# An opening with blank products, spare buffers and loads by need; the third group's norm one group of turns later

## The chip, the cores and the metric

The kernel runs on one core of one Trainium2 chip. The metric is device time in microseconds (us) of one execution of the whole program. Engines are named as in the profile: PE (TensorE matmul) with PEld (its weight loads), DVE (VectorE), ACT (ScalarE), POOL (GpSimd) and SP (SyncE, which only issues DMAs here; SPq in the profile). Each engine runs its own instructions in order and waits on semaphores for the others.

## The reference

Two layers over x of 64 sequences x 32 rows x 256 features, with a context of 64 x 257 x 256. Each of six steps adds a function of the normed x to x:

```
x = x + L0_xattn(layernorm(x), ctx)      # 16 heads of 16, rotary positions, causal window
x = x + L0_attn(layernorm(x))            # causal self attention, rotary positions
x = x + L0_ffn(layernorm(x))             # one product, rows scaled and rounded to fp8
x = x + L1_xattn(layernorm(x), ctx)      # full attention over 257 context rows
x = x + L1_attn(layernorm(x))            # gated mixer with a running sum
x = x + L1_ffn(layernorm(x))             # shared expert and the best 2 of 8 experts
```

The change lies in the first step. With everything else cut away it is

```
m = mean(x); v = var(x); n = (x - m) / sqrt(v + 1e-5)
q = rope(split(n   @ q_w.T + q_b)) * 16 ** -0.5
k = rope(split(ctx @ k_w.T + k_b));  v = split(ctx @ v_w.T + v_b)
e = exp(scores - max(scores)),  scores = q . k  for keys at or before the query, among the first 32
x = x + merge((e / sum(e)) @ v) @ o_w.T + o_b
```

where rope turns each head's halves (a, b) into (a cos - b sin, a sin + b cos).

## The kernel before

**Groups and turns.** The 2048 rows of x form four groups (NG) of 512; a group is four tiles (NT) of 128 rows, that is of four sequences. The two attentions of layer 0 run in one pipeline over `order`, eight items n: four groups of the cross attention, then four of the self attention. Each n has four turns t, and a turn handles one tile. The list `line` carries tiles through five stages, one per turn: `scores`, `sums`, `turned` with `context`, `by_feature`, `project`. In the turns of n the kernel also makes ready the next item, `after` (n + 1): its keys, queries and values, one projection per turn (`rotated`) and two value products (`values`). In the same turns the rows of n + 2 are normed by the generator `side` (`norm_steps`), which is advanced by `prepare`, and are transposed by `opened` at t = 3. All instructions of this stage are kept in program order on every engine, so the Python order is the order of each queue.

**Norm.** `norm_steps` takes the statistics on DVE (four bn_stats, four aggregates), starts an inverse square root with three integer steps (ve, half, r0), refines it with three Newton rounds and writes y = (x - m) r, a pair of tiles at a time. With `eng` vector a Newton round is three small DVE operations; without it, four small POOL operations. Each `yield` is a place where the caller can put other work.

**Rotary exchange.** `rotated(it, i, c)` makes half c of the keys (i = 1) or queries (i = 0): PE fills `ps_qk`, DVE writes `part` (times sine), SP issues four DMAs that copy `part` into `far` with its halves of 32 partitions swapped, `near` (times cosine) comes from DVE for n = 0 and from ACT and POOL for later n, and the function returned adds near and far on POOL into `kT` or `qT`. There are two buffers each of near and part (rings n0, n1 and p0, p1), three of far. `spread_keys` then writes `kT` into the block form `kb`, three heads on ACT and one on POOL, for half a group at a time.

**Values.** `values` writes two tiles to `v`, SP stores them to `v_rows` in HBM, and `blocks` loads them back as `vb` in four DMAs per half group. The parts of `vb` off the blocks must be zero: four clears (`clear`) at the start, two on DVE and two on POOL.

**Opening.** Before the loop (L500 to L537) the kernel loads x and the weights (`first_loads`, a generator whose steps are taken by `next(loads)`: three before the loop, then one in most turns), norms group 0, makes its keys, queries and values, norms group 1 and loads group 0's `vb`. Group 1's transposes (`opened(after)`) come in the turn (0, 0), group 2's in (0, 3). For n = 0 group 2's Newton rounds are on DVE; in later n on POOL. SP issues all loads but two, in program order, so a transfer behind an issue that waits is issued late.

Of the kernel before, what the change touches and what calls it, by code (L numbers as in the profile page):

```python
# [7 lines left out]
F32 = mybir.dt.float32  # L8
# [8 lines left out]
P = 128  # L17
# [48 lines left out]
def perceiver_kernel(ctx: ExitStack, tc: tile.TileContext, a: dict, out: bass.AP):  # L66
# [57 lines left out]
    def norm_steps(g, eng=None, apart=False, ts=range(NT), by_act=False):  # L124
# [18 lines left out]
        r = r0.bitcast(F32)  # L143
        for _ in range(3):
# [102 lines left out]
    def small_attentions(layers, first_loads, decode, sides, load_layer1, layer1):  # L247
# [30 lines left out]
        def clear(vb, engine):  # L278
            engine.memset(vb.rearrange("p b h g e -> p (b h g e)"), 0.0)
# [25 lines left out]
        def rotated(it, i, c):  # L305
# [19 lines left out]
            part = part_([P, GT], "part")  # L325
# [8 lines left out]
            near = near_([P, GT], "near")  # L334
# [166 lines left out]
        eye = sb.tile([P, S], BF16, tag="eye", name="eye")  # L501
        loads = first_loads()
# [4 lines left out]
        next(loads)  # L507
        for half in range(2):
            clear(vbs[0][half], vector)
            clear(vbs[1][half], gpsimd)  # L510
# [4 lines left out]
        adds = [rotated(it, 1, 0)]  # L515
# [3 lines left out]
        steps = norm_steps(order[1][1], vector, apart=True)  # L519
        next(steps)  # L520
        adds.append(rotated(it, 1, 1))
# [4 lines left out]
        adds.append(rotated(it, 0, 1))  # L526
        adds[1]()
# [4 lines left out]
        for pair in range(2):  # L532
            values(it, pair)
        after["y"] = finish(steps)
        for half in range(2):
            blocks(it, half)
        now = it  # L537


        line = [None] * 5  # L540
        adds = []
        layer1_loads = load_layer1()
        for n in range(len(order) + 1):
# [4 lines left out]
            kvT = coming = None  # L548
            if n + 2 <= last:
                side = norm_steps(order[n + 2][1], None if n else vector, apart=True)  # L550
            else:
                side = sides

            def prepare(at):
                if n + 2 <= last and at:
                    try:
                        next(side)
                    except StopIteration as end:
                        return end.value

            for t in range(NT):
# [9 lines left out]
                if t == 0:  # L571
# [9 lines left out]
                else:  # L581
                    y = prepare(t % 2 == 1)
                    adds.append(rotated(after, *((1, 0), (1, 1), (0, 0), (0, 1))[t]))
                if line[3]:
                    by_feature(line[3])
                prepare(t % 2 == 0)
# [13 lines left out]
                elif t % 2 == 0:  # L600
                    values(after, t // 2)
                    if (n, t) == (0, 0):
                        opened(after)
                elif t == 3:
                    for half in range(2):
                        blocks(after, half)
                    if n + 2 <= last:
                        coming = group(n + 2, kvT)
                        coming["y"] = y
                        opened(coming)  # L610
# [10 lines left out]
                if t == 0 and n + 2 <= last:  # L621
                    kvT = fetch(n + 2)
                elif n < 3:
# [1444 lines left out]
```

## Time and profile before

| what | us |
|---|---|
| runs, median (lowest to highest of 3) | 906.89 (904.85 to 907.39) |
| the profiled execution, its own time | 907.43 |
| its span from first to last instruction | 905.7 |
| first PE product | 8.16 |
| score products of groups 0, 1, 2 begin (mask product of the turn t = 0) | 30.85, 51.62, 75.51 |
| PE busy in 0 to 20, 20 to 40 | 11.84, 16.78 |
| PE busy in 104 to 128 (24.0) | 23.61 |

A profile line of an instruction gives start, duration, engine, source line, operation, output<-inputs, shape and count, and in brackets the idle time of the engine before it and what ended that time. L107 and L119 are helpers through which all engines' operations and all matrix products pass, so groups are told apart by the names of the tiles. A chain line gives start, duration and the engine or transfer that the end was waiting for at that time. The time of a DMA is from its issue to its landing.

### The profile page before, as it was taken

To read this page: it belongs to the slowest core of one execution; us is meant where nothing else is said; L and a number is where in the kernel's file an instruction comes from. 1 tells how busy PE (TensorE), PEld (TensorE's weight loads), DVE (VectorE), ACT (ScalarE), POOL (GpSimd) and SP (SyncE) were. 2 spreads that over 40 slices of the span, in tenths; PEclk is the share of its full clock that TensorE was granted. 3 is DMA by queue.
4 is the path that set the end of the run, shared out by engine and by line. 5 is a ranking of instruction groups with operands and counts; after the bars stand their busy time and mean duration, and the time that the engine had idled before them with its cause. 6 is when DMAs were issued, how large, how long until landed. Compare 5 with 4: busy or idle time off the path is not lost.

```text
span 905.7 us, 22825 instructions
## 1 busy us (share of the span) xinstructions
PE 852.7 (94%) x8699; PEld 587.2 (65%) x8699; DVE 583.9 (64%) x1706; ACT 437.8 (48%) x1129; POOL 505.7 (56%) x992
## 2 busy tenths in 40 slices
PE   6899999979899999999999999999898889999997
PEld 3466666656456666666666666565566548888886
DVE  7887777897677677774785766778765861111116
ACT  2567666654555554554555546655544232222224
POOL 3477777864774757564664648555652353555430
PEclk9999999999999999999999999999899999999999
DMA  7455433543110111111011113000001056776668
GB/s 241 136 143 136 100 90 104 135 118 106 54 54 4 52 54 54 54 54 54 7 49 54 54 54 100 3 1 2 25 25 36 24 160 193 238 237 232 215 188 284
DMA packets 66926, 88.77 MB, mean 98 GB/s; under 512 B 32480, under 2 KB 50688, under 8 KB 64768
## 3 DMA queue, kind: packets, MB, share of 16 engines
q1 hardware_dynamic: 63264, 77.73, 28.6%
q0 software_dynamic: 3456, 9.44, 3.1%
q8 instruction: 69, 1.13, 0.5%
q14 instruction: 41, 0.34, 0.1%
q10 hardware_dynamic: 96, 0.13, 0.1%
HBM read 65.78 MB, written 13.11 MB: 87 GB/s over the span
## 4 chain that ended last, share of the span: by engine, by line
PE 71%; DVE 15%; POOL 4%; ACT 4%; issue 3%; DMA 2%; SPq 0%; DVEq 0%; POOLq 0%; ACTq 0%
PE ps_v L119 12%; PE ps_o L119 11%; PE ps_k L119 10%; PE ps_h L119 7%; PE ps_t L122 7%; PE ps_qk L119 4%; PE ps_s L119 4%; PE ps_p L119 3%; PE ps_so L119 2%; PE ps_q L119 2%; PE pair_bank L119 1%; DVE y L107 1%; POOL sq L107 1%; ACT e L107 1%; PE psT L122 1%
## 5 line engine op out<-in xcount | busy, mean ns | idle before, releaser
L107 ACT ACTIVATE e<-e,xnm 128x257 f32<-128x257 f32 x256 | 127.2, 499 | 50.9 <-DVE xnm L107 41.0
L107 DVE CUSTOM_DVE_ANT_0 e<-ps_s,mask 128x257 f32<-128x257 f32 x256 | 93.5, 421 | 49.8 <-PE ps_s L119 49.5
L119 PE MATMUL ps_k<-ct,w_w_l1x 128*128 128x512 f32 x256 | 122.3, 600 | 1.6 <-ACT yT L107 0.6
L119 PE MATMUL ps_v<-w_w_l1x,ct 128*128 128x256 f32 x512 | 122.3, 382 | 0.0
L107 POOL TENSOR_SCALAR e<-e,xsm 128x256 f32<-128x256 f32 x256 | 121.3, 492 | 0.0
L122 PE MATMUL ps_t<-cst,e 128*128 128x128 f32 x640 | 102.7, 284 | 7.7 <-DVE eT L107 6.8
L107 DVE COPY eT<-ps_t 128x512 f32<-128x512 f32 x124 | 85.2, 687 | 28.6 <-PE ps_t L122 28.4
L119 PEld LDWEIGHTS ps_v<-w_w_l1x,ct 128*128 128x128 f32 x512 | 94.5, 193 | 11.0 <-issue 0.2
L107 ACT ACTIVATE kT<-ps_k,vec 128x512 f32<-128x512 f32 x64 | 44.0, 688 | 101.0 <-PE ps_k L119 100.7
L107 POOL TENSOR_TENSOR x<-x,rows 128x256 f32<-128x256 f32 x96 | 71.0, 755 | 37.3 <-ACT y L107 18.0
L122 PEld LDWEIGHTS ps_t<-cst,e 128*128 128x128 f32 x640 | 71.9, 142 | 26.2 <-DVE eT L107 7.7
L107 ACT ACTIVATE hTr<-ps_h,w 128x256 f32<-128x256 f32 (+1 forms) x80 | 31.4, 449 | 106.0 <-issue 82.7
L107 DVE TENSOR_TENSOR og<-ps_o,b 128x512 f32<-128x512 f32 (+1 forms) x20 | 12.8, 639 | 105.6 <-PE ps_o L119 105.6
L119 PEld LDWEIGHTS ps_k<-ct,w_w_l1x 128*128 128x128 f32 x256 | 44.6, 190 | 41.3 <-issue 35.2
L1811 POOL DMA_INDIRECT r_rows<-og,lv x36 | 35.5, 986 | 61.0 <-DVE og L107 56.1
L119 PE MATMUL ps_h<-ygT,w 128*128 128x256 f32 (+1 forms) x320 | 67.5, 365 | 0.1
L107 ACT COPY v<-ps_v 128x512 f32<-128x512 f32 x80 | 46.4, 581 | 39.2 <-PE ps_v L119 39.1
L119 PE MATMUL ps_o<-w,hTr 128*128 128x256 f32 x288 | 65.3, 379 | 0.0
L107 POOL TENSOR_TENSOR last<-e,xsm 128x4 f32<-128x4 f32 x64 | 12.9, 202 | 88.6 <-DVE xsm L107 88.6
L119 PEld LDWEIGHTS ps_h<-ygT,w 128*128 128x128 f32 x320 | 56.2, 194 | 6.6 <-issue 0.3
L119 PEld LDWEIGHTS ps_o<-w,hTr 128*128 128x128 f32 x288 | 54.5, 190 | 7.2
L107 ACT ACTIVATE kb<-kT,cst 128x256 f32<-128x256 f32 x96 | 45.4, 512 | 25.7 <-POOL kT L107 24.0
(210 smaller groups left out, 1667.1 us busy)
## 6 DMA issues: line engine op xcount, KB each, us to landing
ct<-in_ctxT SPq DMA_DIRECT2D x16, 1024.0 KB, 5.6
w<-in_ew SPq DMA_DIRECT2D x20, 514.0 KB, 4.1
w<-in_ew SPq DMA_DIRECT2D x20, 512.0 KB, 3.8
far<-part SPq DMA_DIRECT2D x126, 64.0 KB, 2.5
v_rows<-v SPq DMA_DIRECT2D x16, 256.0 KB, 2.3
vb<-v_rows SPq DMA_DIRECT2D x64, 64.0 KB, 2.3
r<-r_rows SPq DMA_DIRECT2D x8, 512.0 KB, 7.2
b<-in_eb SPq DMA_DIRECT2D x20, 128.0 KB, 3.7
```

The costliest lines, as they stand in the source:

```text
L107: ins = getattr(self.engine, name)(*args, **kw)
L119: return kept(nc.tensor.matmul(ps, **args))
L122: return kept(nc.tensor.transpose(ps, src, eye))
L1811: wrote = nc.gpsimd.indirect_dma_start(out=r_rows, out_offset=bass.IndirectOffsetOnAxis(ap=write_i[:, at : at + 1], axis=0), in_=o[:, i, : ...
```

## The change

The opening starts with 14 products of a zeroed bf16 tile `blank` into the PSUM bank b5, which nothing reads. All four clears of `vb` are on POOL. Both halves of group 0's keys are projected before its transposes; the first two `part` and `near` tiles are in the tiles that scores and exponentials use later (sc0, sc1, e0, e1), not in their rings. Group 1's norm gets one more place to pause. The loads of x2, w3, one bias row and the fp8 weights come after group 0's values; x3 and the later rows and weights come in later turns, and group 2's context in the turn (0, 1). The second half of group 0's `vb` is loaded in (0, 1). In the turns of n = 0 the adds stand first in each turn; group 1 is transposed in (0, 1). Group 2's statistics are taken in (0, 2), its Newton rounds in (0, 3), now on POOL, its y in (1, 0) and (1, 1), and its transposes in (1, 1).

```diff
@@ -121,7 +121,7 @@
     def turn(ps, src, eye):
         return kept(nc.tensor.transpose(ps, src, eye))
 
-    def norm_steps(g, eng=None, apart=False, ts=range(NT), by_act=False):
+    def norm_steps(g, eng=None, apart=False, ts=range(NT), by_act=False, split=False):
 
         x = xs[g]
         n, t0 = len(ts), ts[0]
@@ -141,6 +141,8 @@
         r0 = small.tile([P, n], I32, tag="r0", name="r0")
         vector.tensor_scalar(r0, half, -1.0, float(0x5F3759DF), ALU.mult, ALU.add)
         r = r0.bitcast(F32)
+        if split:
+            yield
         for _ in range(3):
             sq = small.tile([P, n], F32, tag="sq", name="sq", bufs=6)
             rn = small.tile([P, n], F32, tag="rn", name="rn", bufs=6)
@@ -275,8 +277,8 @@
             scalar.copy(mk, cst[:, at : at + S][:, None, :].to_broadcast([P, 8, S]))
             masks.append(mk)
 
-        def clear(vb, engine):
-            engine.memset(vb.rearrange("p b h g e -> p (b h g e)"), 0.0)
+        def clear(vb):
+            gpsimd.memset(vb.rearrange("p b h g e -> p (b h g e)"), 0.0)
 
         def fetch(n):
             layer, g = order[n]
@@ -322,7 +324,8 @@
                 return tile_.rearrange("p (b q) -> p b q", q=S)
 
             bias = vec[:, v0 + 2 * i + c : v0 + 2 * i + c + 1]
-            part = part_([P, GT], "part")
+            spare = (it["n"], i) == (0, 1)
+            part = sb.tile([P, GT], F32, tag=f"sc{c}", name="part") if spare else part_([P, GT], "part")
             vector.scalar_tensor_tensor(
                 by_seq(part), by_seq(ps), bias, by_place(sn), ALU.add, ALU.mult
             )
@@ -331,7 +334,7 @@
             for at in range(0, P, S):
                 queue = scalar if (it["n"], i, c) == (0, 0, 1) and at >= 2 * S else sync
                 queue.dma_start(out=far[at : at + S, :], in_=part[at ^ S : (at ^ S) + S, :])
-            near = near_([P, GT], "near")
+            near = sb.tile([P, GT], F32, tag=f"e{c}", name="near") if spare else near_([P, GT], "near")
             if it["n"] > 0:
                 scalar.activation(near, ps, AF.Identity, bias=bias)
                 gpsimd.tensor_tensor(by_seq(near), by_seq(near), by_place(cs), ALU.mult)
@@ -499,31 +502,35 @@
 
         kT_all = sb.tile([P, 2, GT], F32, tag=wide[4], name="kT")
         eye = sb.tile([P, S], BF16, tag="eye", name="eye")
+        blank = sb.tile([P, GT], BF16, tag="e2", name="blank")
+        vector.memset(blank, 0.0)
+        idle = psum.tile([P, GT], F32, tag="b5", name="idle")
+        for _ in range(14):
+            mm(idle, lhsT=blank[:, 0:P], rhs=blank, start=True, stop=True)
         loads = first_loads()
         next(loads)
         it = group(0, fetch(0))
         next(loads)
         after = group(1, fetch(1))
-        next(loads)
-        for half in range(2):
-            clear(vbs[0][half], vector)
-            clear(vbs[1][half], gpsimd)
+        for vb in vbs[0] + vbs[1]:
+            clear(vb)
         scalar.copy(ident_bf, ident)
         mask(0)
         it["y"] = finish(norm_steps(order[0][1], vector))
         it["kb"] = [None, None]
-        adds = [rotated(it, 1, 0)]
+        adds = [rotated(it, 1, c) for c in range(2)]
         opened(it)
         mask(1)
         vector.tensor_tensor(eye, ident[:, 0:S], ident[:, 64 : 64 + S], ALU.add)
-        steps = norm_steps(order[1][1], vector, apart=True)
+        steps = norm_steps(order[1][1], vector, apart=True, split=True)
         next(steps)
-        adds.append(rotated(it, 1, 1))
+        next(steps)
         adds[0]()
         for part in range(2):
             spread_keys(it, 0, 0, part)
         adds.append(rotated(it, 0, 0))
         adds.append(rotated(it, 0, 1))
+        next(steps)
         adds[1]()
         for part in range(2):
             spread_keys(it, 0, 1, part)
@@ -531,14 +538,14 @@
             add()
         for pair in range(2):
             values(it, pair)
+        next(loads)
+        next(loads)
+        blocks(it, 0)
         after["y"] = finish(steps)
-        for half in range(2):
-            blocks(it, half)
         now = it
 
-
         line = [None] * 5
-        adds = []
+        adds, side = [], None
         layer1_loads = load_layer1()
         for n in range(len(order) + 1):
             if n > 0:
@@ -546,17 +553,22 @@
             if after is not None:
                 after["kb"] = [None, None]
             kvT = coming = None
+            earlier = side
             if n + 2 <= last:
-                side = norm_steps(order[n + 2][1], None if n else vector, apart=True)
+                side = norm_steps(order[n + 2][1], apart=True)
             else:
                 side = sides
 
-            def prepare(at):
-                if n + 2 <= last and at:
+            def prepare(count):
+                y = None
+                for _ in range(count if n + 2 <= last else 0):
                     try:
                         next(side)
                     except StopIteration as end:
-                        return end.value
+                        y = end.value
+                return y
+
+            ahead, behind = ((0, 1, 0, 1), (1, 0, 1, 0)) if n else ((0, 0, 0, 1), (0, 0, 1, 0))
 
             for t in range(NT):
                 if line[2]:
@@ -568,7 +580,7 @@
                     elif after is not None:
                         kb_now = (after, 0, t - 2)
                 due, adds = adds, []
-                if t == 0:
+                if t == 0 or n == 0:
                     for add in due:
                         add()
                     due = []
@@ -579,11 +591,17 @@
                 if after is None:
                     next(layer1, None)
                 else:
-                    y = prepare(t % 2 == 1)
+                    if n == 1 and t == 0:
+                        next(earlier)
+                    elif n == 1 and t == 1:
+                        after["y"] = finish(earlier)
+                    y = prepare(ahead[t])
                     adds.append(rotated(after, *((1, 0), (1, 1), (0, 0), (0, 1))[t]))
+                    if n < 2 and t == 1:
+                        opened(after)
                 if line[3]:
                     by_feature(line[3])
-                prepare(t % 2 == 0)
+                prepare(behind[t])
                 if n + 2 > last:
                     next(side, None)
                     next(side, None)
@@ -599,15 +617,16 @@
                     next(layer1, None)
                 elif t % 2 == 0:
                     values(after, t // 2)
-                    if (n, t) == (0, 0):
-                        opened(after)
                 elif t == 3:
                     for half in range(2):
                         blocks(after, half)
                     if n + 2 <= last:
                         coming = group(n + 2, kvT)
-                        coming["y"] = y
-                        opened(coming)
+                        if n > 0:
+                            coming["y"] = y
+                            opened(coming)
+                if (n, t) == (0, 1):
+                    blocks(now, 1)
                 line[0] = scores(now, t) if n <= last else None
                 if (n, t) == (last, NT - 1):
                     pair_pool.close()
@@ -618,9 +637,9 @@
                     context(line[2])
                 if line[1]:
                     sums(line[1])
-                if t == 0 and n + 2 <= last:
+                if t == (0 if n else 1) and n + 2 <= last:
                     kvT = fetch(n + 2)
-                elif n < 3:
+                elif n < 3 and (n, t) != (0, 0):
                     next(loads, None)
                 elif n >= last - 2:
                     next(layer1_loads, None)
@@ -646,12 +665,15 @@
         sync.dma_start(out=xs[1], in_=x_view[1])
         yield
         sync.dma_start(out=xs[2], in_=x_view[2])
+        yield
         sync.dma_start(out=w_cur[:, 3], in_=a["w_l0x"][:, 3])
         row_load(R_XO0)
+        sync.dma_start(out=raw, in_=a["w_fp8"])
+        yield
         sync.dma_start(out=xs[3], in_=x_view[3])
         yield
-        sync.dma_start(out=raw, in_=a["w_fp8"])
-        for at in (R_AO0, R_FF, R_XO1, R_GO):
+        row_load(R_AO0)
+        for at in (R_FF, R_XO1, R_GO):
             yield
             row_load(at)
         for i in range(0, 4, 2):
```

## The prediction

> **What bounds the kernel now.** I read the page first, then busy time by stretches, then the opening in order of time, then the chain of waits up to 60 us.
>
> ```profile
> span 905.7 us, 22825 instructions
> ...
> PE 852.7 (94%) x8699; PEld 587.2 (65%) x8699; DVE 583.9 (64%) x1706; ACT 437.8 (48%) x1129; POOL 505.7 (56%) x992
> ...
> PE 71%; DVE 15%; POOL 4%; ACT 4%; issue 3%; DMA 2%; SPq 0%; DVEq 0%; POOLq 0%; ACTq 0%
> ```
>
> ```profile
> 20.00:30.80 10.80, 7.58 (x32) 4.71 (x30) 9.68 (x28) 4.85 (x12) 5.40 (x7) 1.00 0.53 139
> 30.80:51.60 20.80, 20.29 (x285) 12.74 (x284) 17.13 (x45) 14.32 (x32) 11.96 (x13) 0.92 0.46 126
> 51.60:75.20 23.60, 22.95 (x369) 16.11 (x368) 19.69 (x45) 15.44 (x36) 17.32 (x28) 1.00 0.51 134
> ...
> 80.00:104.00 24.00, 23.67 (x375) 16.03 (x372) 18.52 (x44) 15.72 (x36) 17.34 (x28) 1.00 0.54 134
> ```
>
> The columns are stretch, length, then busy time of PE, its weight loads, DVE, ACT, POOL, then granted clock. From 51.6 us on PE works 97 to 99% of each group's 23.6 to 24 us, so whatever PE starts earlier there is kept to the end. Spare time exists only before: 8.16 us until the first product, 3.2 us of the stretch 20 to 30.8, and a clock of 0.92.
>
> ```profile
> 8.16 3.75 PE L119 MATMUL ps_qk<-kvT,w_w_l0x 128*128 128x512 f32 x4 [8.16 <-DMA kvT<-in_ctx32T]
> ...
> 22.53 1.96 PE L119 MATMUL ps_qk<-kvT,w_w_l0x 128*128 128x512 f32 x4
> 24.33 1.99 PE L119 MATMUL ps_v<-w_w_l0x,kvT 128*128 128x256 f32 x8
> 27.93 0.78 PE L122 MATMUL psT<-cst,y 128*128 128x128 f32 x4 [1.61 <-DVE y L107]
> 30.24 0.68 PE L122 MATMUL psT<-cst,y 128*128 128x128 f32 x4 [1.53 <-ACT near L107]
> 30.85 0.41 PE L119 MATMUL pair_bank<-mk,eye 64*32 64x256 bf16 x8
> ```
>
> ```profile
> 14.64 3.52 DMA far<-part
> ...
> 18.29 1.28 POOL kT L107
> ...
> 26.95 2.55 issue
> 29.50 0.69 ACT near L107
> ```
>
> The same projection (four records) takes 3.75 us at the start and 1.96 later: PE starts at half speed, though the granted clock reads 1.00 there; durations decide. It is slow again after the idle time of 26.3 to 30.2: the clock row of 31 to 34 us is 0.50. The first score product of group 0 stands at 30.85; it waits for the exchange far (3.52 us instead of the median 2.3, behind 369 GB/s of loads), for the rotations one after another, and for PE's transposes of group 1, held by DVE.
>
> **Part 1, blank products.** PE's first instruction now needs only a DVE clear of 128x256 words; 2048 took 1.76 us, so under 0.3: start about 1.6 us. No row shows a 128x512 bf16 product. A 128x256 one is 0.13 (ps_ff, eight in 1.04 from 206.55), and bounds it below; four times that, twice the columns at half clock, is 0.52 above. So 14 take 1.8 to 7.3 us and end at 3.4 to 8.9. I take eight slow and six fast (8x0.52 + 6x0.26 = 5.7), end 7.3, before kvT lands at 8.03; the upper end costs 0.9 us of start. In this trace PE needed about 4.2 us of work to leave half speed (8.16 to 12.4, where the transposes quicken) and fell back after some 4.4 us with 0.8 us of work in them. The hole 7.3 to 8.16 is shorter. The Trainium skill, "TensorE: Matmul & The Clock Gate", What's actually happening, says the watching window is 3.4 us and free-running; by its 0.427 us a slow product all 14 would end at 7.6, and an unlucky window only shifts how many are slow.
>
> **Part 2, order up to the first score product.** PE: both key projections 2x1.8 from 8.16 to 11.8, transposes 1.3 to 13.1, ACT's second copy 0.58 to 13.7, queries 3.60 to 17.3, values 3.63 to 20.9, group 1's key and value projections 1.73 each to 24.4. The DVE clears (2x1.76) leave before the norm; four POOL clears (4x1.81 from 0.74) end at 8.0, and POOL was idle until 18.29. The spare part/near buffers remove two waits of queries on keys (1.34 <- DMA far, 0.50 and 0.60 <- POOL kT). Exchange side: part of the first keys at 10.3, its four issues (0.6 each) 11.1 to 13.5 with x2, w3, row and x3 no longer in front, landing 15.4; keys' adds 16.8 and 19.1; the queries' issues end 20.3 (two on ACT), landing 22.3, adds 22.4 and 23.7. So the first score product comes at 24.4, PE's own time, against 30.85: **-6.4**. Group 1's transposes (1.3) move behind it, and group 2's move out of group 0's turns, so PE's work in those turns stays equal.
>
> **Part 3, group 0's turns.** What is late next is SP's queue, which is full. ACT copies the values at 21.9; then SP issues v_rows (2), x2, w3, row, raw to 24.2, four vb 1.9, far of group 1's first keys 2.4 (to 28.6), v_rows 0.5, far 2.4, the other four vb 1.9, kvT 0.4, far of the first queries 2.4: to 36.2, landing about 38.2. On POOL behind it: query add 1.28 (39.5), key spread 0.5, and now group 2's Newton steps, twelve of 0.285 in pitch as the steps at 56.78 to 60.06 (43.4). They were DVE's before (nine at 0.2). Behind them wait the near product 1.28 (44.7) and the second query add (46.0), which group 1's first scores need. These stood at 51.62, so 5.6 of the 6.4 are left: **+0.8**. PE alone would be ready at 44.1.
>
> **Part 4, group 1's first turns.** In the chain before, DVE runs without a break from 49.78 (part) to 56.70, then near and cT on ACT, then ps_p at 58.85: 9.07 us. Added to it: the second pair of y, 2x0.39 = 0.79, and two yT copies (1.07) between near and cT: 10.9. It starts when the first pair of y is done, and that needs the Newton steps of 43.4. Rows bound it: free, y takes 0.8 (part at 44.2, ps_p at 55.1); blocked by POOL it does not.
>
> ```profile
> 43.44 1.26 DVE L107 TENSOR_SCALAR y<-x,mv,rn 128x256 f32<-128x256 f32 x2
> ...
> 62.41 1.25 DVE L107 TENSOR_SCALAR y<-x,mv,rn 128x256 f32<-128x256 f32 x2
> ```
>
> Both pairs began while a POOL add ran (42.95, 61.92) and waited for its end; here near and add follow at once, so y could end at 46.4 and ps_p come at 57.3. That is 3.7 or 1.5 before 58.85; I take the middle, 2.6: **+3.0**. The skill's "SBUF — State Buffer", Who interferes with whom, speaks against moving work to GpSimd here: whoever starts first holds the shared port for the whole instruction. By that rule alone POOL, in order on its own engine, wins, and the sum would be -1.5. PE's 1.3 us of transposes lies inside this wait.
>
> Loads that are put later: x3 is issued about 36.7 and must be there for group 3's statistics at about 45; w_l0a comes one or two slots later, three turns ahead of use. Both free; uncovered, x3 costs what it is late beyond 8 us (median landing 7.9 in the crowded opening).
>
> **Sum** -6.4 + 0.8 + 3.0 = -2.6 on the profiled execution's 907.43 (span 905.7 plus 1.7 around it) is 904.8. The median of the runs, 906.89, lies 0.54 below that execution, so I forecast 904.3 for the median.
>
> **Rivals.** A: everything is carried. POOL gets to near and the add before the Newton steps bind, or far lands earlier; then the half-clock stretch (3.02 against 1.88, 1.08 against 0.64, small ones: 1.7) is saved too, against 1.3 for transposes in a full group: -6.8, 900.1. For it: PE is the bound in 71% of the chain; against: SP's and POOL's queues above. B: the products don't warm PE (idle before kvT, or the wrong window). The first key pair and transposes run slow: 1.9 + 0.7, the whole chain of v_rows and SP starts 2.6 later, net 0: 906.9. Against it: the 4.2 us seen. C, slower: the exchange of the first queries lands as slowly as loads do, because kvT (512 KB) now stands right before it on SP; before it stood 3.3 us ahead. Price: x's median landing 7.9 less 2.3 = 5.6, straight down POOL to part 4, and PE idles 44 to 50, long enough to halve its clock again as at 30.7, 2.1 more: -2.6 + 7.7 = +5.1, 912.0. It eats the gain from 2.6 us of lateness and is measurably slower from 5.3. Against it: only one load of 512 KB is in flight there, and far at 37.20, 3.3 us behind the same load, showed no delay.
>
> **How the numbers follow.** Forecast (-1 to -5) 0.50, A 0.20, B 0.12, C 0.18. A change of 0.3% (2.7 us) is about what can be told from none: three fifths of the forecast's share and A are beyond it, 0.50; the rest of the forecast and B within, 0.32; C slower, 0.18. The likeliest case alone spans 901.9 to 905.9. The range reaches into A and past B: 900.3 to 908.0.
>
> **What would show it.** First projection in about 1.9 us at 8.2; first score product at 24 to 25; no clock row under 1.0 before 60; PE idle 1 to 2 us before group 1's first scores with POOL's add as releaser; y of group 2 with a mean over 0.6 us; ps_p near 56. Wrong if PE runs half clock at 8 to 12, if far after kvT lands later than 4 us, or if group 1's first turns take no longer than before.

## The result and the profile after

| | before | after |
|---|---|---|
| median of 22 runs each (lowest to highest), us | 906.29 (903.96 to 908.89) | 908.59 (906.03 to 913.52) |
| ratio, 95% interval | | 1.0026 [1.0014, 1.0037] |
| profiled execution, us (span) | 907.43 (905.7) | 908.40 (906.6) |
| score products of groups 0, 1, 2 begin (t = 0) | 30.85, 51.62, 75.51 | 24.69, 45.87, 76.59 |
| those of group 1's second turn | 56.28 | 56.66 |
| last ps_so product begins | 881.34 | 882.29 |

The change made the kernel slower by 0.26%: inside the 0.3% that the prediction called no change, but with an interval that excludes no change at all. 904.3 was forecast, with 900.3 to 908.0 as the range. The opening gained 6.2 us as said, and 5.75 of them stood until 45.87; between there and 76.59 all was lost, and 1.1 more. From 76.59 to the end nothing of that difference moves (0.95 at the last ps_so).

The page of the kernel after: span, busy time of the engines, and the chain that ended last.

```profile
span 906.6 us, 22850 instructions
...
PE 854.8 (94%) x8713; PEld 587.2 (65%) x8713; DVE 581.3 (64%) x1696; ACT 437.9 (48%) x1129; POOL 510.7 (56%) x1006
...
PE 69%; DVE 17%; ACT 5%; POOL 3%; issue 3%; DMA 2%; SPq 1%; DVEq 0%; ACTq 0%; POOLq 0%
```

Busy time by stretches, after (columns as in the prediction; one row each for the end of the opening, group 0's turns, group 1's turns, and a later group):

```profile
20.00:24.60 4.60, 4.60 (x19) 3.09 (x17) 4.32 (x10) 2.66 (x6) 3.46 (x4) 1.00 0.72 194
24.60:45.80 21.20, 19.15 (x285) 12.05 (x284) 15.11 (x35) 13.48 (x29) 10.67 (x18) 1.00 0.73 198
45.80:76.50 30.70, 25.93 (x377) 17.88 (x376) 24.30 (x54) 17.58 (x41) 20.92 (x36) 0.94 0.41 106
80.00:104.00 24.00, 23.67 (x370) 16.10 (x369) 18.51 (x45) 15.90 (x38) 17.34 (x28) 1.00 0.55 149
```

PE has no idle time left from 20 to 24.6 and its clock is whole up to 45.8. The group that took 23.6 us before with PE 97% busy takes 30.7 now, with 4.8 us idle and a clock of 0.94. The later group is as it was.

The opening in order of time, after:

```profile
1.19 4.78 PE L119 MATMUL idle<-blank 128*128 128x512 bf16 x14 [1.19 <-DVE blank L107]
...
6.44 1.36 DVE L107 TENSOR_SCALAR ve<-mv 128x4 f32<-128x4 f32 x1
...
7.79 3.67 PE L119 MATMUL ps_qk<-kvT,w_w_l0x 128*128 128x512 f32 x8 [1.81 <-DMA kvT<-in_ctx32T]
...
16.19 1.27 POOL L107 TENSOR_TENSOR kT<-near,far 128x512 f32<-128x512 f32 x1 [8.42 <-DVE half L107]
```

Both key projections run at full speed (3.67 for two; 3.75 for one before), and the first add of keys stands at 16.19 instead of 18.29. SP's queue in group 0's turns, after (start, time over the group of issues):

```profile
24.93 1.86 SPq L107 DMA_DIRECT2D vb<-v_rows  x4
26.90 3.96 SPq L107 DMA_DIRECT2D far<-part  x4
30.95 0.53 SPq L107 DMA_DIRECT2D v_rows<-v  x1
31.59 2.42 SPq L107 DMA_DIRECT2D far<-part  x4
34.05 2.10 SPq L107 DMA_DIRECT2D vb<-v_rows  x4
36.25 1.20 SPq L107 DMA_DIRECT2D kvT<-in_ctx32T  x1
37.56 2.42 SPq L107 DMA_DIRECT2D far<-part  x4
...
41.27 2.41 SPq L107 DMA_DIRECT2D far<-part  x4
```

The last two rows are the exchanges of group 1's first and second queries. The first ends its issues at 39.98; 36.2 was forecast. The queue is full from 24.93 on. Two rows are long: the first far takes 3.96 instead of 2.42, and kvT 1.20 instead of 0.40 to 0.45. The whole starts 0.7 later than forecast. The view of SP's waits (us in total, times, longest) has three lines for landings between 24.9 and 31 us, 1.7 us together, all of loads issued from 23.29 to 24.83; for kvT's row it names no wait:

```profile
SPq L107 <- DMA raw<-in_w_fp: 1.1, 1, 1.1
...
SPq L107 <- DMA rows<-in_rows: 0.4, 1, 0.4
...
SPq L107 <- DMA w_w_l0x<-in_w_l0x: 0.2, 1, 0.2
```

What follows, on POOL, DVE and PE:

```profile
41.68 1.27 POOL L107 TENSOR_TENSOR qT<-near,far 128x512 f32<-128x512 f32 x1 [3.11 <-DMA far<-part]
...
46.46 0.20 POOL L107 TENSOR_TENSOR rn<-sq,rn 128x4 f32<-128x4 f32 x1
46.61 1.26 POOL L107 TENSOR_TENSOR near<-near,cst 128x512 f32<-128x512 f32 x1
46.69 2.67 DVE L107 TENSOR_SCALAR y<-x,mv,rn 128x256 f32<-128x256 f32 x2 [3.95 <-POOL rn L107]
47.95 1.26 POOL L107 TENSOR_TENSOR qT<-near,far 128x512 f32<-128x512 f32 x1
...
49.26 0.68 PE L119 MATMUL pair_bank<-kb,qT 64*32 64x128 f32 x16 [2.87 <-POOL qT L107]
49.28 0.74 DVE L107 SCALAR_TENSOR_TENSOR part<-ps_qk,vec,cst 128x512 f32<-128x512 f32 x1
...
59.95 1.13 PE L119 MATMUL ps_p<-w_w_l0x,cT 128*128 128x256 f32 x4 [1.36 <-ACT cT L107]
```

The chain is plain: the exchange lands late (add 41.68), the twelve Newton steps end at 46.66, DVE is idle for 3.95 us and its pair of y then takes 2.67 us across two POOL operations, and the second add, at the end of POOL's row, holds the second half of group 1's scores: PE is idle for 2.87 us in the middle of them. Its clock then falls:

```profile
49.00:52.00 3.00, 2.74 (x53) 2.19 (x54) 3.00 (x7) 1.87 (x5) 1.80 (x3) 0.50 0.49 116
52.00:53.00 1.00, 1.00 (x5) 0.83 (x5) 1.00 (x2) 0.60 (x2) 1.00 (x2) 0.89 0.43 102
```

PE has 2.74 us of work in these 3 us, at half clock (0.50). From group 1's first score products to those of its second turn 10.8 us pass; it was 4.7 before.

### The profile page after: what moved, and what is told of

Same layout as the page of the kernel before. It is cut to its first block, busy times and chain, and to the rows that moved or that the text cites. A ratio compares the mean times of both kernels' runs of the same rounds, so it can differ in the third digit from the quotient of the medians.

```text
span 906.6 us, 22850 instructions
## 1 busy us (share of the span) xinstructions
PE 854.8 (94%) x8713; PEld 587.2 (65%) x8713; DVE 581.3 (64%) x1696; ACT 437.9 (48%) x1129; POOL 510.7 (56%) x1006
## 4 chain that ended last, share of the span: by engine, by line
PE 69%; DVE 17%; ACT 5%; POOL 3%; issue 3%; DMA 2%; SPq 1%; DVEq 0%; ACTq 0%; POOLq 0%
PE ps_v L119 12%; PE ps_o L119 11%; PE ps_k L119 10%; PE ps_h L119 7%; PE ps_t L122 7%; PE ps_s L119 4%; PE ps_qk L119 4%; PE ps_p L119 3%; PE ps_so L119 2%; ACT e L107 2%; DVE y L107 2%; PE ps_q L119 2%; POOL sq L107 1%; PE pair_bank L119 1%; DVE x L107 1%
```

## The experiments

"L" is the version of experiment 6. All ratios are to the kernel before, run beside them on the same chip. The first four columns are where the score products begin in the profiled execution (t = 0 of group 0; t = 0 and t = 1 of group 1; t = 0 of group 2).

| run | group 0 | group 1 | its t = 1 | group 2 | median | ratio, 95% interval |
|---|---|---|---|---|---|---|
| before | 30.85 | 51.62 | 56.28 | 75.51 | 906.29 | |
| after | 24.69 | 45.87 | 56.66 | 76.59 | 908.59 | 1.0026 [1.0014, 1.0037] |
| opening_only | 25.69 | 54.36 | 59.37 | 78.17 | 906.87 | 0.9991 [0.9976, 1.0006] |
| move_only | 31.24 | 50.85 | 57.13 | 76.70 | 908.37 | 1.0010 [0.9992, 1.0028] |
| no_blank | 24.96 | 47.36 | 58.79 | 78.72 | 911.09 | 1.0046 [1.0026, 1.0067] |
| act_loads | 26.39 | 47.25 | 58.60 | 78.52 | 909.49 | 1.0028 [1.0012, 1.0043] |
| late_loads | 25.85 | 46.42 | 57.99 | 76.76 | 907.93 | 1.0016 [1.0001, 1.0031] |
| dve_newton | 24.69 | 48.93 | 54.46 | 74.31 | 907.86 | 1.0009 [0.9992, 1.0026] |
| newton_early | 24.69 | 44.96 | 55.57 | 74.33 | 905.94 | 0.9991 [0.9973, 1.0008] |
| late_newton (L) | 26.39 | 46.73 | 55.67 | 75.21 | 903.43 | 0.9965 [0.9946, 0.9985] |
| q_first | 24.69 | 52.23 | 57.77 | 77.33 | 907.95 | 1.0017 [1.0000, 1.0034] |
| late_q | 24.69 | 52.30 | 57.84 | 77.48 | 907.43 | 1.0016 [0.9999, 1.0032] |
| late_blank | 24.69 | 46.09 | 57.13 | 75.89 | 904.88 | 0.9982 [0.9969, 0.9995] |
| late_q_blank | 24.69 | 51.60 | 57.18 | 77.12 | 908.40 | 1.0026 [1.0011, 1.0041] |
| vb_later | 24.69 | 45.49 | 56.35 | 75.40 | 905.88 | 0.9992 [0.9977, 1.0008] |
| late_vb | 24.69 | 44.74 | 57.01 | 75.92 | 905.74 | 0.9992 [0.9979, 1.0005] |
| newton_vb | 26.29 | 46.14 | 58.37 | 77.41 | 906.65 | 0.9995 [0.9976, 1.0014] |
| newton_vb_x3 | 24.69 | 44.98 | 54.92 | 74.85 | 906.94 | 0.9999 [0.9987, 1.0011] |
| late_x3 | 24.69 | 44.76 | 52.09 | 72.02 | 904.97 | 0.9977 [0.9955, 0.9998] |
| newton_x3 | 26.38 | 46.08 | 56.29 | 75.94 | 906.92 | 1.0008 [0.9995, 1.0020] |

The marks come from one execution and the median from 12 (after 22, no_blank 8), and executions of one kernel differ in PE's mean granted clock: of late_x3's twelve, the one with 0.989 took 901.68 and the one with 0.971 took 911.48. So a mark that moved 1 us is a hint; where marks and medians disagree the median decides.

**1. The two halves of the change alone.** opening_only keeps the new opening and puts group 2's norm back where it was:

```diff
-                side = norm_steps(order[n + 2][1], apart=True)
+                side = norm_steps(order[n + 2][1], None if n else vector, apart=True)
-            ahead, behind = ((0, 1, 0, 1), (1, 0, 1, 0)) if n else ((0, 0, 0, 1), (0, 0, 1, 0))
+            ahead, behind = (0, 1, 0, 1), (1, 0, 1, 0)
...
-                        if n > 0:
-                            coming["y"] = y
-                            opened(coming)
+                        coming["y"] = y
+                        opened(coming)
```

> The new opening (blank products, spare buffers, clears on POOL, loads by need), but group 2 is normed in group 0's turns with its Newton steps on DVE and transposed in (0, 3), as before the change. Theory M (the move of group 2 eats the opening's gain): first scores of group 0 at 24.7 as in the changed kernel, first scores of group 1 near 46.5 without a hole in the middle, then 4.7 us to the next scores as before; 4 to 5 us under the kernel before, 902. Rival S (the late exchange behind SP's queue alone eats it, wherever group 2 is normed): first scores of group 1 complete at 49 or later, 906 or more.

move_only is the kernel before with only group 2's norm and transposes moved as in the change.

> The opening and the loads of the kernel before; only group 2's norm, Newton steps and transposes are moved as in the change. M: the move costs by itself 3 to 5 us, because y waits for the Newton steps on POOL and then for two POOL adds: 909 to 911. S: without the late exchange the move is nearly free, 906 to 907.5.

Neither half explains the result by itself. The opening alone starts its scores 5.2 us earlier and has lost it all by group 1. One reason is that x2, loaded by need, is late for the old place of the norm:

```profile
28.86 1.40 DVE L107 BATCH_NORM_STATS2 st<-x 128x6 f32<-128x256 f32 x4 [2.03 <-DMA x<-in_x]
...
36.85 3.78 PE L119 MATMUL ps_qk<-yT,w_w_l0x 128*128 128x512 f32 x4 [3.18 <-ACT yT L107]
```

DVE waits 2.03 us for x2 and then has the norm's own steps, up to 34.25, in front of the rotation of group 1's second keys. PE later waits 3.18 us for yT, which ACT copies behind that rotation, and its projection (3.78 instead of 1.88) shows half clock. That the opening needs a later norm is argued from these rows, not shown: by the runs the move as it was made costs on top of the opening, for opening_only lies 1.7 us under the changed kernel, with intervals that do not touch. move_only's marks say 1.2 us at group 2, its interval holds no change: the price of the move alone is not settled.

**2. Blank products.** no_blank issues one instead of 14.

```diff
-        for _ in range(14):
+        for _ in range(1):
```

> The changed kernel with one blank product and not 14. If the 14 are what makes PE fast in the opening: the first four projections' records at about 0.94 us each until 12.2, transposes later, first scores of group 0 at 26.5 to 27 and not at 24.7. If SP's queue and POOL set the end of group 0's turns, group 1's first scores come equally late and the time changes by less than 2 us: 909 to 910.5. If PE were the bound of these turns, 911.

The first pair of key projections takes 5.41 us instead of 3.67:

```profile
7.42 5.41 PE L119 MATMUL ps_qk<-kvT,w_w_l0x 128*128 128x512 f32 x8 [5.63 <-DMA kvT<-in_ctx32T]
```

The first scores move only 0.27 us, group 1's 1.5 us, and the median lies 2.5 us over the changed kernel's (the intervals of the two ratios overlap a little). Part 1 of the prediction stands: the products help, by some 2 us if one goes by the medians; the overlap leaves the size open.

**3. The loads in front of SP's exchanges.** act_loads issues x2, w3, the row and raw from ACT's queue, ahead of group 0's query products; late_loads leaves x2 and w3 and puts the row and raw behind x3, in the turn (0, 2).

```diff
 # late_loads
-        row_load(R_XO0)
-        sync.dma_start(out=raw, in_=a["w_fp8"])
         yield
         sync.dma_start(out=xs[3], in_=x_view[3])
+        row_load(R_XO0)
+        sync.dma_start(out=raw, in_=a["w_fp8"])
         yield
```

> The changed kernel with the loads of x2, w3, the bias row and the fp8 weights issued on ACT's queue after the second mask (about 14.4 us) and not on SP between the stored values and vb. S: SP gets 3.5 us back, the exchange of group 1's first queries lands at 38 to 39 and not at 41.6, and the whole stretch behind it comes 3 us earlier: 905. M alone (the Newton steps and y on POOL's chain): the chain shifts with the exchange as well, but keeps its length; 905 to 907. If the loads now crowd group 0's own exchange, its first scores come 1 to 2 us later than 24.7.

> The changed kernel with the bias row and the fp8 weights loaded in (0, 2), behind x3, and not before vb: SP's issues of group 1's first key exchange then wait for no landing (8 DMAs before them are older ones). S: these four issues take 2.4 and not 4.0 us, the exchange of the first queries is issued 2.4 us earlier and lands at 39.2 and not at 41.6; everything behind it shifts by 2.4: second query add at 46.8, next scores at 54.2, 906. If the turns are held by something else (PE, DVE, vb), the landing moves and the scores don't.

In act_loads the exchange of group 1's first keys issues in 2.43 us, without a wait, so the 3.96 is the landing of those loads. The issues of group 0's own exchanges, now beside the loads, take 11.14 us instead of 8.89, and the first scores slip to 26.39, as the expectation had it, but not for its reason:

```profile
14.16 5.40 PE L119 MATMUL ps_qk<-yT,w_w_l0x 128*128 128x512 f32 x8 [0.68 <-ACT yT L107]
```

PE's query projection took 1.70 us longer than the changed kernel's (3.70), and PE had no idle time from there to the scores. late_newton and newton_x3, whose loads are not in front of those exchanges, show the same 5.40 and the same mark. So this profile does not price the crowding; the median shows no gain. late_loads has 2.96 in that row, and its median is 0.7 us lower, which is within what can be told. That the row gets shorter does not hold in L: with the same two loads out of the way it takes 4.10 there and waits for x2 and w3.

**4. Group 2's Newton steps on DVE** again (dve_newton, one line: `None if n else vector`), their place as in the change.

> The changed kernel with group 2's Newton steps on DVE (nine of 0.2 us in (0, 3)) and not on POOL. M: POOL's near product and second query add move 3.4 us forward, y no longer waits for them; the hole before the second half of group 1's first scores shrinks from 2.9 to about 1.5 us, 2 to 3 us under the changed kernel: 906. S: the add still waits for the exchange, whose part is now 1.8 us later on DVE; gain under 1 us: 908.

The hole inside the scores is gone (48.93 to 54.46), at the price of a later start; group 2's mark is 2.3 us better than after, the median 0.7, within its interval.

**5. Newton one turn earlier** (newton_early), still on POOL: the statistics in (0, 1), the steps in (0, 2), where POOL would otherwise be waiting for the exchange.

```diff
-            ahead, behind = ((0, 1, 0, 1), (1, 0, 1, 0)) if n else ((0, 0, 0, 1), (0, 0, 1, 0))
+            ahead, behind = ((0, 1, 0, 1), (1, 0, 1, 0)) if n else ((0, 0, 1, 0), (0, 1, 0, 0))
```

> The changed kernel with group 2's statistics in (0, 1) and its Newton steps on POOL in (0, 2) and not in (0, 3); y and the transposes stay. Theory M (POOL's Newton steps ahead of the near product and the second query add hold both y and the scores): Newton ends near 40.7, y ends near 45 and not at 49.4, the second query add near 47.5 and not at 49.2, the hole in group 1's first scores is 1.5 us and the next scores begin near 52.5 and not at 56.66; 3 to 4 us under the changed kernel, 905. Rival S (the late exchange alone): the second query add stays at 49, gain under 1 us, 908.

```profile
41.74 1.68 DVE L107 TENSOR_SCALAR y<-x,mv,rn 128x256 f32<-128x256 f32 x2
...
47.33 1.26 POOL L107 TENSOR_TENSOR qT<-near,far 128x512 f32<-128x512 f32 x1 [2.33 <-DMA far<-part]
...
48.65 0.45 PE L119 MATMUL pair_bank<-kb,qT 64*32 64x128 f32 x16 [3.17 <-POOL qT L107]
```

y ends at 43.4 instead of 49.4, and the median falls 2.65 us, its interval clear of the changed kernel's. The hole stays, though: the second add comes only 0.6 us earlier and now waits for its exchange. POOL's lateness had covered a late landing.

**6. Both 3 and 5** (late_newton, that is late_loads and newton_early together).

> Both together: Newton steps in (0, 2) and the bias row and fp8 weights behind x3. M and S together: first query exchange lands at 39.2, second query add ends near 45.5, no hole in group 1's first scores (they begin near 45), the next scores at 50.5 to 51.5, which is 5 us under the kernel before at that point: 902 to 903. If this is not under the kernel before, neither cause is the one that eats the gain.

903.43, ratio 0.9965 [0.9946, 0.9985]: faster than the kernel before, and the lowest median of the 18 variants. Its interval overlaps that of newton_early, whose marks are no worse, so what late_loads adds to it is not shown. Its profile still has the hole (second add at 49.12, PE idle 3.17), but its clock does not fall, as busy time by stretches shows:

```profile
40.00:50.00 10.00, 6.72 (x94) 4.29 (x78) 7.61 (x15) 6.62 (x16) 6.53 (x13) 1.00 0.72 220
50.00:60.00 10.00, 8.59 (x152) 6.15 (x153) 7.85 (x22) 5.17 (x12) 6.79 (x19) 1.00 0.64 173
```

**7. More blank products.** late_blank is L with 22 instead of 14.

> The same version with 22 blank products instead of 14, so that TensorE is busy from 1.2 us to the landing of the first context and does not stand idle from 5.97 to 7.79. Theory H (the hole of 1.8 us lets the clock fall in some executions, as the clock of 0.86 between 8 and 20 us in two profiles): first score products at 24.4 to 24.9 in every profile, no clock row under 1.0 before 24 us, and a median 0.5 to 1.5 us lower than 903.4. Theory V (those differences are scatter of the profiled execution, or the gate falls later whatever was before): the median stays at 903 to 904, or rises by what the products overrun the landing.

Both profiles with 22 products have the first scores at 24.69, while those with 14 lie at 24.69 or, in six of fifteen, at 25.7 to 26.4. The hole between the products and kvT is closed, though the first projection starts at 8.79 and 8.18 instead of 7.42 in L. The median does not fall (904.88 to 903.43). The hole explains the spread of that mark only in part at best. In two of the six (opening_only, late_loads) the first key projections run slow (5.27 and 5.26 us), after holes of 2.20 and 2.29, the longest of the fifteen. In the other four the query projection does (5.30 to 5.40), and in newton_vb, one of these, PE has no idle time in front of kvT: the products end at 7.32 and the projection begins at 7.44.

**8. The failed term: SP's queue in front of group 1's first query exchange.** q_first puts both vb's second half and group 2's kvT behind it; late_q does the same to L, late_q_blank with 22 products as well. The edit does one thing more: with the context fetched at t = 2, the turn (0, 1) takes the next load, so x3 comes in front of that exchange (at 33.72 in q_first).

```diff
-                if (n, t) == (0, 1):
+                if (n, t) == (0, 2):
                     blocks(now, 1)
...
-                if t == (0 if n else 1) and n + 2 <= last:
+                if t == (0 if n else 2) and n + 2 <= last:
                     kvT = fetch(n + 2)
```

> The changed kernel, but the second half of group 0's vb and group 2's context are issued behind the exchange of group 1's first queries instead of in front of it. Theory Q (the term that failed is SP's queue in front of that exchange): its four issues start 2 to 3.4 us earlier than 37.56, it lands at 38 to 39.5 instead of 41.6, Newton ends near 44 instead of 46.66, y of group 2 and the second query add come some 2 us earlier, group 1's second turn begins 2 us before 56.66, and the median falls by 1 to 2.5 us under the changed kernel's 908.6. Theory N (GpSimd's own work, twelve Newton steps in front of near and add, is the whole cost): the second add moves with the first, but y still waits behind both GpSimd operations, the stretch from first to second score products stays near 10 us, and the median stays within 0.7 us of 908.6.

> The version with the earlier Newton steps and the later bias row and fp8 loads, and in addition vb's second half and group 2's context issued behind the exchange of group 1's first queries. Theory Q: first query add at 40 or earlier, the add of the second queries (49.12 there, waiting for its exchange) 2 us earlier, group 1's second turn before 54.5, median 900.5 to 902.5. Theory N: the Newton steps were the cost and are already gone, so the median stays at 903 to 904.

> Both of the last two edits together. If they are independent, the gains add: 899.5 to 902 by theories Q and H, 903 to 904 by N and V.

These miss, in an instructive way; from q_first:

```profile
45.42 3.78 PE L119 MATMUL ps_qk<-kvT,w_w_l0x 128*128 128x512 f32 x4 [3.46 <-DMA kvT<-in_ctx32T]
```

The context for group 2's keys now lands late: PE is idle for 3.46 us and runs the projection at half clock. The exchange itself, behind x3, is issued 3.1 us earlier (34.42), but its add starts at 40.88, only 0.8 us earlier and 4.05 us after its last issue. L loses its gain (late_q, 907.43 for 903.43). vb_later therefore moves vb alone (the first of the two edits), late_vb does so in L.

> The changed kernel with one move: the four loads of the second half of group 0's vb behind the exchange of group 1's first queries; group 2's context keeps its place in front of it. Theory Q: SP reaches that exchange 2 us earlier (35.4 to 35.6 instead of 37.56), the first query add starts at 39 to 40 instead of 41.68, Newton, y and the second query add come 1.5 to 2 us earlier, and group 2's key projection does not wait for its context as it did when that was moved too; median 906 to 907.5. Theory L (the landing, not the place in the queue, sets that add): the exchange is issued earlier but lands no earlier than 41, and the median stays within 0.7 us of 908.6.

> The version with earlier Newton steps and the later bias row and fp8 loads (903.43 by its runs) plus the same one move. Theory Q: the second query add, 49.12 there and waiting for its exchange, comes at 47 to 47.5, group 1's second turn by 54.5, median 901 to 902.5. Theory L: 903 to 904.5. If the median comes back at 905 or more with the same marks as that version, 903.43 was partly luck of its runs.

```profile
34.37 2.41 SPq L107 DMA_DIRECT2D far<-part  x4
...
39.43 1.26 POOL L107 TENSOR_TENSOR qT<-near,far 128x512 f32<-128x512 f32 x1 [1.24 <-DMA far<-part]
...
40.30 0.45 SPq L107 DMA_DIRECT2D x<-in_x  x1
40.86 2.41 SPq L107 DMA_DIRECT2D far<-part  x4
...
44.46 1.65 DVE L107 TENSOR_SCALAR y<-x,mv,rn 128x256 f32<-128x256 f32 x2 [2.10 <-POOL rn L107]
...
48.12 1.42 POOL L107 TENSOR_TENSOR qT<-near,far 128x512 f32<-128x512 f32 x1 [2.48 <-DMA far<-part]
```

One move of four DMA issues brings the first query add from 41.68 to 39.43 and the median from 908.59 to 905.88; the interval, [0.9977, 1.0008], is clear of the changed kernel's. This shows the failed term, though of the 2.7 us the mark of group 2 has 1.2 (75.40 for 76.59). But the second add again waits for its exchange: 4.85 us from the last issue (43.27) to the add, where the first exchange of the changed kernel needed 1.7 (39.98 to 41.68). In L the move gains nothing (905.74, the intervals overlap).

**9. The load in front of the second exchange.** x3 (512 KB) is issued right before it (in L with the bias row and raw between). newton_vb joins 5 and vb_later; newton_vb_x3 also puts x3 behind the second exchange; late_x3 and newton_x3 do that to L and to 5.

```diff
-                elif n < 3 and (n, t) != (0, 0):
+                elif n < 3 and (n, t) not in ((0, 0), (0, 2)):
                     next(loads, None)
...
                 elif t == 3:
+                    if n == 0:
+                        next(loads)
                     for half in range(2):
                         blocks(after, half)
```

> Newton steps of group 2 one turn earlier, and vb's second half behind the exchange of group 1's first queries: the two edits that alone gave 905.94 and 905.88. If each takes away its own term (GpSimd's twelve steps in front of y; SP's queue in front of the exchange), the sum is below both, 903 to 904.5. If both only free the same GpSimd stretch, and group 1's second query add waits for the landing of its own exchange with x3 in front of it (4.3 us from the last issue to the add in one, 4.8 in the other), nothing adds up: 905 to 906.5, second add at 47 to 48.5 still with a DMA as releaser.

> The same, and the load of x3 (512 KB) behind the exchange of group 1's second queries instead of in front of it. Theory X (that exchange lands late because a load stands in front of it, as the third rival had it for the first queries): from its last issue to the add 1.8 to 2.6 us instead of 4.3 to 4.8, second add at 44.5 to 45.5, no idle time over 1.5 us inside group 1's first scores, group 1's second turn by 53.5, median 1 to 2.5 us under the run without it. Theory Y (late for other traffic): the add stays at 47 or later and the median within 0.7 us. If group 3's statistics then wait for x3, that shows as a DVE wait on a DMA near 50.

> The version of 903.43 with x3, the bias row and the fp8 weights behind the exchange of group 1's second queries. Theory X: second add at 47 or earlier instead of 49.12, median 901 to 902.5. Theory Y: 903 to 904.5.

> The version with the earlier Newton steps (905.94) and one more move: the load of x3 behind the exchange of group 1's second queries; vb and all other loads keep their place. Theory X: with GpSimd free and no load in front, the second add starts at 43.5 to 45.5 instead of 47.33, the idle time inside group 1's first scores falls from 3.2 to under 1.5 us, group 1's second turn begins by 53.5 instead of 55.57, group 2's first scores by 73.5 instead of 74.33, and the median is 903 to 905. Theory Y: add at 47 or later, median within 0.7 us of 905.9. As in the run before, group 3's statistics may now wait for x3; if that takes the gain back, it stands as a wait of DVE for a DMA of over 3 us and group 1's second turn stays after 54.5.

newton_vb shows that the two cures do not add: each frees POOL, and both then wait for the second exchange. In the seven profiles where POOL waits for it with x3 in front, the add comes 6.9 to 7.8 us after x3's issue, wherever the exchange's own issue stands (dve_newton 40.00 to 46.92, newton_early 40.03 to 47.33, vb_later 40.30 to 48.12, late_vb 41.00 to 48.37, late_blank 41.09 to 48.90, late_newton 41.96 to 49.12, newton_vb 42.69 to 50.39); the first exchange of q_first, behind x3 as well, 7.2. With x3 behind it, from newton_x3:

```profile
46.84 1.26 POOL L107 TENSOR_TENSOR qT<-near,far 128x512 f32<-128x512 f32 x1 [0.49 <-DMA far<-part]
...
50.07 1.41 DVE L107 BATCH_NORM_STATS2 st<-x 128x6 f32<-128x256 f32 x4 [4.64 <-DMA x<-in_x]
```

The exchange now lands 1.65 us after its last issue (45.19), 1.60 in newton_vb_x3: the load in front was what made it land late. But the gain goes straight to a new wait: group 3's statistics stand 4.64 us waiting for x3 on DVE (4.96 in newton_vb_x3), ahead of the softmax, and the medians do not fall. late_x3 has the best marks of all, 72.02 for group 2; its second exchange is issued 3.5 us earlier than in newton_x3, and x3 with it (wait 2.49), but 1.7 of this is the slow query projection in newton_x3's profile. Its median, 904.97, is nevertheless not below L's 903.43, with overlapping intervals.

## Why the prediction was wrong

**What bounds the kernel** was right: what PE keeps at 76 us is kept to the end (+1.08 there, +0.95 at the last product).

**Part 1** was right in kind; 14 products took 4.78 us rather than 5.7 and ended at 5.97, and kvT landed at 7.79. Rival B fell (experiment 2), though in two of the fifteen profiles with 14 products the first key projections ran slow as it had them (experiment 7).

**Part 2** was right: 24.69 for 24.4, and in nine of the fifteen profiles. One thing in it was not seen: the clears on POOL, costed at nothing, held a DVE operation of four words per row for 1.36 us, and the second half of group 0's transposes waited 0.97 for DVE.

**Part 3** has the step that failed: "to 36.2, landing about 38.2". The landing after the last issue was sized rightly (2.0 forecast, 1.7 measured). The issue itself was 3.8 us late, because I counted each DMA by the time that issues take when nothing holds them. The loads by need had been put in front of the exchanges, and the queue stood until they had landed: 1.5 us in the first far. kvT took 0.8 us more, for which the view names no wait; the six issues up to raw took 3.0 us for the 2.3 that I counted; the rest lies in vb and in small gaps. act_loads shows the first of these by its absence, vb_later the worth of the place in the queue. That group 1's scores still began at 45.87, as forecast (46.0), was an accident: their first half needs only the first add, which I had not separated. The second half waited until 49.26 for the second add, forecast to end at 46.0.

**Part 4** then left its own bounds. y was bounded by 46.4 on the side "blocked by POOL"; it ended at 49.36, 3.0 later, and ps_p came at 59.95 instead of 57.3 at the latest. This is Part 3's lateness carried down POOL's row (Newton end 46.66 for 43.4). The mechanism, y locked behind near and add, was the one priced: 2.67 us for the pair. The Trainium skill's "SBUF — State Buffer", Who interferes with whom, which was weighed there with -1.5, spoke for the dearer end, and the trace agrees with it. Newton in another place (experiment 5) removes this term: 2.65 us by the medians.

**Not in the sum at all** was the hole of 2.87 us and the half clock after it: 2.1 us in rival C, nothing in the forecast. The stretch from group 1's to group 2's scores grew by 6.83 us (30.72 for 23.89); Part 4 granted 3.0.

**Rival C** was the right kind, but at the other exchange. In the changed kernel the first exchange, behind kvT, landed 1.7 us after its last issue, about as fast as an exchange with no load in front (1.6). In eight other versions where POOL waited for it, it came 1.7 to 3.9 us after, still far from the 7.9 that C feared. The second, behind x3, came no sooner than 6.9 us after that load's issue, and 1.6 us after its own last issue with x3 behind it. In the changed kernel POOL was as late (x3 issued at 40.65, near ended at 47.87), so there this cost nothing. It is what stood next once one cure was made; with it gone too, the wait for x3 stood next, so no version brought the 6 us back.

**What stays open.** Why L has the lowest median although its profile shows the same hole. Its clock did not fall there, but that execution took 905.16, more than L's median, and L is the lowest of many variants; only further executions could tell how much is chance. How the 4.3 us between 904.3 and 908.59 divide between Part 3's lateness and the hole with its half clock is not settled either, since each cure brought some 2.7 us and both together no more. And of the 2.3 us by which the medians differ, the marks explain 1.0; the runs of after had a mean clock of 0.9807 against 0.981 to 0.983 in the runs of before beside the experiments, which goes the same way, but no run isolates it.

## What to carry to other kernels

When loads are put off until they are needed, cost them in the queue where they now stand: the full issuing queue here passed late landings on to the exchanges behind it, so count issues with the landings of those ahead, not by their length alone. Work moved onto an idle engine is free only while that engine's next input is late; ask what it is waiting for and put the moved work into that wait, not behind it. And when one cure works and a second one does not add to it, look for what both of them uncovered.

## What the hardware showed that was not expected

- A hole in PE's work of about 3 us can halve the clock or not: after one of 2.87 us it read 0.50 from 49 to 52 us, after one of 3.17 in newton_early 0.72 from 48 to 53, after one of 3.17 in late_newton 1.00. One of only 1.87 in newton_vb_x3 was followed by 0.50 from 48 to 51. In the ten profiles with such a hole of 2.87 to 5.04 inside group 1's first scores late_newton's is the only clock that did not fall to 0.50. The Trainium skill's "TensorE: Matmul & The Clock Gate", What's actually happening, has a free-running window of 3.4 us; that both outcomes occur at one length would fit it.
- A DVE operation on 128x4 elements took 1.36 us while POOL cleared a tile (the next of its kind 0.17), and two y of 0.36 each took 2.67 us beside two POOL operations of 1.26.
- The last of four 64 KB transfers landed up to 4.9 us after its issue when x3 (512 KB) was issued right in front of them (vb_later). It landed 1.7 (the changed kernel) to 3.9 us (late_blank) after when kvT (512 KB) was, and 1.6 with neither (newton_vb_x3).
